# Page numbers kept in registers, a probability read moved behind the key pages, and two block transposes moved behind a projection's additions

## The chip, the cores and the metric

The kernel runs on one core of one Trainium2 chip. The core has a matrix engine (TensorE, PE in the profile), a vector engine (VectorE, DVE), a scalar engine (ScalarE, ACT), a general engine (GpSimd, POOL) and a synchronization engine (SyncE, SP) that here only issues transfers and loads registers. Each engine works through its own queue in order; engines wait for each other, and for transfers, through semaphores. The metric is the time of one execution in device microseconds (us); lower is better.

## The reference

A transformer-like block in two layers, all in float32, for 8 sequences of 128 tokens with 512 features:

```python
x = x + ffn0(cond0(x))      # per-sequence 512x512 weight; then base matrix + mixture of 8 low-rank experts, top 2
x = x + ffn1(cond1(x))      # attention over a paged cache; then 64 experts of rank 8, top 16

def cond1(x):               # 32 query heads, 8 key/value heads, head size 128
    q, k, v = x @ Wq.T, x @ Wk.T, x @ Wv.T
    q, k = rope(rmsnorm(q) * qw, pos), rope(rmsnorm(k) * kw, pos)   # pos = cache_seqlens + token
    kc, vc = k_cache[block_table], v_cache[block_table]             # 16 pages of 32 keys a sequence
    scores = q @ concat(kc, k).T / sqrt(128)                        # 512 cached + 128 own keys
    scores = where(cached key index < cache_seqlens, scores, -1e30)
    return (softmax(scores) @ concat(vc, v)) @ Wo.T
```

## The kernel before

The first layer runs first (to about 130 us), the last layer's feed-forward part partly at the end. In between stands a main loop over 64 units, and the change lies there. A unit is one sequence and one key/value head with its four query heads. Units are ordered by step: step `st` is one sequence and one pair of key/value heads, and its two units are `u = 2*st` (first turn) and `u = 2*st + 1` (second turn). All engines are scheduled by hand: the order in which the program writes the instructions is the order in each engine's queue. `iteration(u)` writes one turn of the loop, and it works on several units at once:

- `scores(u, h)` for the four heads h (L439: 512 cached keys, L442: 128 own keys), into one of two PSUM buffers that alternate; `mask_exp` (DVE L452 masks and finds the row minimum, ACT L463 takes the exponential); `normalize` (DVE L468 takes the reciprocal of the row sum, POOL L469 scales the row).
- `blocks(u, h)` (DVE L474) transposes a head's probabilities in blocks of 32x32 into the buffer `pb`; `blocks_qk(u + 2, u)` (DVE L425) does the same for the rotated queries and keys of unit u + 2, in the same buffer. There is one `pb`: it is written for a unit after the exchange of the unit before has read it.
- `exchange_out(u)` (L486) writes `pb` to a buffer px in DRAM, two transfers from SP and two from ACT, 400 KB each. `exchange_in(u - 1)` reads px back in the transposed arrangement: `qkb` (L1000, 320 KB: queries and keys of unit u + 1) and `pT` (L1003, 1280 KB: probabilities of unit u - 1). `heads_qk` (ACT L1010) then makes `qkT` for the next unit's scores. `values(u - 2)` (PE L1023) multiplies the probabilities with the cached values at the end of the turn.
- `gather(st + 1, ...)` reads the key pages of the next step, 16 pages of 32 KB, eight in each turn. For each page SP loads the page's number from SBUF into a register (L192, TENSOR_LOAD) and issues the transfer with it (L193, packets of 256 bytes). Five pages stand ahead of `exchange_in`, three behind it. `gather_v` reads values from POOL.
- `project` (PE L262) computes the query, key and value projections of later units by a seven-product scheme, three or four products a turn. In the slots of heads 1, 2 and 3 it takes `slots[h - 1]`; DVE adds each product to its partial sums (L265). Turns with u%4 = 3 or 1 take products 1, 2, 6 and 7, the others 4, 5 and 3. Product 5 (slot of the third head, h = 2) needs two additions, product 2 one.
- `output(u - 3, h)` (PE L1148) multiplies earlier results with the output weight into the PSUM bank `y`; `add_output` (DVE L1217) adds it to the accumulators, the late part after the last `blocks`. `rotate(u + 3)` (DVE L329 to L347) follows it, and it waits for the factors `rs` that `norms` computes on ACT (L311) and POOL (L315, L317).

POOL also carries weight sums (L163, L1098), loads of weights (`load_q`, L153, in turns with u%16 from 7 to 12, between the scaling of the third and of the fourth head) and the gathers of values. Within one head's slot, PE's order is scores, output, projection. In the slot of the third head DVE's order before the change is: mask step of head 2, reciprocal of head 1, `blocks_qk`, `blocks(u, 0)`, the projection's additions; the mask step of head 3 follows.

Of the kernel before, what the change touches and what calls it, by code (L numbers as in the profile page):

```python
# [17 lines left out]
B = 8  # L18
# [8 lines left out]
PAGES, PSIZE, NPP = 64, 32, 16  # L27
# [3 lines left out]
GH = 2  # L31
# [27 lines left out]
def adaln_ffn_kernel(  # L59
# [25 lines left out]
    nc = tc.nc  # L85
# [20 lines left out]
    pg = const.tile([1, B * NPP], I32, name="pg")  # L106
# [70 lines left out]
        for i, to in parts:  # L177
            nc.gpsimd.dma_start(out=wo_t[:, to], in_=wo[hf, i])

    kv_t = {}  # L180

    def gather(step, first=0, end=NPP):
        hf, b = divmod(step, B)
        if first == 0:
            kv_t[step] = (
                kvp.tile([P, NPP, GH, PSIZE], F32, tag="kt", name=f"kt_{step}"),
                kvp.tile([P, LC, GH * D], F32, tag="vt", name=f"vt_{step}", bufs=3),
            )
        kt, vt = kv_t[step]
        for j in range(first, end):  # L190
            at = b * NPP + j
            page = nc.sync.value_load(pg[0:1, at : at + 1])  # L192
            nc.sync.dma_start(  # L193
                out=kt[:, j, :, :].rearrange("p g t -> p (g t)"),
                in_=kc[hf, ds(page, 1)].rearrange("o p f -> p (o f)"),
            )
# [30 lines left out]
    NU = len(units)  # L227
# [176 lines left out]
    mask_t, px_t, qkb_t = {}, {}, {}  # L404
# [18 lines left out]
    def blocks_qk(u, w):  # L423

        nc.vector.transpose(  # L425
            pb_t[w][:, :, PW:].rearrange("p i (h a) -> p h i a", a=32),
            qk_t.pop(u).rearrange("p h t d -> p h (t d)").rearrange(
                "p h (i a) -> p h i a", a=32
            ),
        )  # L430
# [35 lines left out]
    def normalize(u, h):  # L466
        den = den_t.pop((u, h))
        nc.vector.reciprocal(den, den)  # L468
        nc.gpsimd.tensor_scalar(p_t[u, h], p_t[u, h], den, 1.0, ALU.mult, ALU.mult)  # L469

    def blocks(u, h):

        w = (LC + 1) * 32
        nc.vector.transpose(  # L474
            pb_t[u][:, :, h * w : (h + 1) * w].rearrange("p i (j a) -> p j i a", a=32),
            p_t.pop((u, h)).rearrange("p (j i a) -> p j i a", i=QD, a=32),
        )

    def exchange_out(u):

        pb = pb_t.pop(u)
        m = dram_x.tile([QD, 32, QD, XW], F32, tag="px", name=f"px_{u}")
        w = XW if u + 2 in range(4, NU) else PW
        for i in range(QD):
            eng = nc.sync if i < QD // 2 else nc.scalar
            eng.dma_start(  # L486
                out=m[:, :, i, :w].rearrange("k b f -> b k f"),
                in_=pb[i * 32 : (i + 1) * 32, :, :w],
            )
        px_t[u] = m  # L490
# [501 lines left out]
    with ExitStack() as l1:  # L992
        wk1 = l1.enter_context(tc.tile_pool(name="l1_1", bufs=1))
        wk2 = l1.enter_context(tc.tile_pool(name="l1_2", bufs=2))

        def exchange_in(u):
            m = px_t.pop(u).rearrange("k b i f -> (k b) i f")
            if u + 2 in range(4, NU):
                qkb = wk1.tile([P, QD, NH * 32], F32, tag="qkb", name=f"qkb_{u + 2}")
                nc.sync.dma_start(out=qkb, in_=m[:, :, PW:])  # L1000
                qkb_t[u + 2] = qkb
            pT = wk1.tile([P, QD, PW], F32, tag=f"pT{u % 2}", name=f"pT_{u}")
            nc.sync.dma_start(out=pT, in_=m[:, :, :PW])  # L1003
            pT_t[u] = pT
# [287 lines left out]
        def room(b):  # L1292
            at = [0]

            def sb(n, shape):
                if n in ("yT", "zg", "zT"):
                    v = room_t[n, b if n != "yT" else b % 2]
                    return v if len(shape) == 2 else v.rearrange("p (c s) -> p c s", c=shape[1])
                at[0] += -(-shape[1] // 8) * 8
                return room_t["small", b % 2][:, at[0] - -(-shape[1] // 8) * 8 :][:, : shape[1]]  # L1300

            def psum(n, shape):
                late = n == "tp" and b >= 4
                t = banks(f"ftp_{b}") if late else bank("kv" if n == "z" else "q", f"f{n}_{b}")
                if len(shape) == 2:
                    return t[:, : shape[1]]
                t = t[:, : shape[1] * shape[2]]
                return t.rearrange("p (c s) -> p c s", c=shape[1])

            return sb, psum  # L1310
# [107 lines left out]
        def iteration(u):  # L1418
            nonlocal room2

            on = lambda v: 0 <= v < NU
            fb = LAST.get(u)
            r, group = u % 16, (u // 16 + 1) * GH
            f = room(fb) if fb is not None else None

            if u % 4 == 3:
                k, j, four = (u + 5) // 4, 0, True
            elif u % 4 == 0:
                k, j, four = (u + 4) // 4, 0, False
            elif u % 4 == 1:  # L1430
                k, j, four = (u + 3) // 4, 1, True
            else:
                k, j, four = (u + 2) // 4, 1, False
# [4 lines left out]
            pages = on(u) and 1 < st + 1 < NQ * B  # L1438
# [1 line left out]
            if pages:  # L1440
                gather(st + 1, first, first + 5)
            if on(u - 1):
                exchange_in(u - 1)
            if pages:
                gather(st + 1, first + 5, end)
            if pages:
                gather_v(st + 1, u % GH * LC // GH, (u % GH + 1) * LC // GH)
            if on(u + 3) and u % GH == 1 and u > 1:
# [38 lines left out]
            for h in range(REP):  # L1487
                if on(u):
                    if (u, h) not in ((1, 0), (1, 1), (2, 0)):
                        scores(u, h)  # L1490
                        mask_exp(u, h)
                    if h > 0 and (u, h) != (1, 1):
                        normalize(u, h - 1)

                    if (u, h) == (1, 2):
                        transpose_qk(3)

                    sums_o(u, h)
                    sums_w(u, h)
                    if 16 <= u < NU - 8 and (r, h) == (2, 3):  # L1500
                        load_o(u // 16, (1, B12))

                    if h == 2:
                        new_pb(u)
                        if u + 2 in range(4, NU):
                            blocks_qk(u + 2, u)
                    if h > 1:
                        blocks(u, h - 2)
                    if h == 1 and u == NU - 5:
                        f_fold()  # L1510
                    if u == NU - 5 and h == 1:
                        t4 = wo_t[:, 6, : 2 * (E1 + HN)].rearrange("p (c n) -> p c n", c=2)
                        fw_t["qa"], qa_steps[:] = quarters_of(
                            fw_t["a"],
                            *quarter_rooms(wo_t[:, 5]),
                            t4[:, :, E1:],
                            t1_room.rearrange("p (c n) -> p c n", c=2),
                        )
                        sa = fw_t["sa"]
                        fw_t["qa"][M1], fw_t["qa"][M2] = (sa[:, c : c + 2, : E1 + HN] for c in (0, 2))  # L1520
                        fw_t["qa"][M4] = t4
                    at = (u - NU + 5, h)
                    if at == (1, 0):
                        nc.vector.tensor_copy(fw_t["qa"][M4][:, :, :E1], fw_t["s"][:, 2:])
                    if at in ((0, 1), (0, 2), (1, 0), (1, 1)):
                        qa_steps.pop(0)()
                    if u in GATED and h == 1:
                        f_add(GATED[u])
                    if u in GATED and h == 2:
                        f_mult(GATED[u])  # L1530
                    if h == 3:
                        z_blocks(u)
                    if h == 2 and u in FIRST:
                        f_turn_of(2 * FIRST[u])
                    if u in REST:
                        if h == 1:
                            f_turn_of(2 * REST[u] + 1)
                        elif h > 1:
                            f_step(REST[u], 2 * h - 4, 2 * h - 3)
                elif u in GATED and u < NU + 2:  # L1540
                    if h == 1:
                        f_add(GATED[u])
                    elif h == 2:
                        f_mult(GATED[u])
                    elif h == 3:
                        z_blocks(u)
                if on(u - 3):
                    output(u - 3, h)
                    sums_a(u - 3, h)
                if u in REST and h == 3:  # L1550
                    f_rest_products(REST[u], 0)
                if h > 0 and slots:
                    project(k, j, slots[h - 1 : h])

                if (u, h) in WHOLE:
                    project_whole(1, *WHOLE[u, h])
            if on(u - 3):
# [19 lines left out]
            if on(u):  # L1577
                blocks(u, REP - 2)
                blocks(u, REP - 1)
                exchange_out(u)  # L1580
            if on(u - 3):
                add_output(u - 3, True)
            if 16 <= u < NU - 8 and r in (0, 1, 2):
                n = u // 16
# [192 lines left out]
```

## Time and profile before

| what | value |
|---|---|
| time, median of 3 executions | 1198.89 us (1198.29 to 1201.55) |
| the profiled execution, its own time | 1203.57 us |
| span of the profiled execution, first to last instruction | 1201.8 us |
| granted TensorE clock in it | 1.00 |
| busy: PE, DVE, ACT, POOL | 99%, 78%, 42%, 64% of the span |
| mean busy share of the DMA engines by queue: SP's, ACT's, POOL's | 53.2%, 13.4%, 12.5% |
| the chain of waits, by engine | PE 82%, DMA 5%, DVE 4%, POOL 4%, issue 2%, SP's queue 2%, ACT 1% |
| transfers, issue to landing (median): kt, px, qkb, pT | 4.8, 5.5, 3.6, 7.3 us |

A group of instructions in the profile is named by its line, engine, operation and tiles (out<-in). "Idle before" is the time for which the engine stood idle just before the instruction, with what ended it. The view of waits lists, for an engine, who waited for whom, the total, the number of times and the longest one. In the order of time, each line gives start, duration, engine, line, operation and tiles; neighbouring instructions of one group are merged (x5 is five of them, and the duration then runs from the first's start to the last's end). SPq is SP's sequencer. Ends of matmuls are modelled.

### The profile page before, as it was taken

The page shows a single profiled execution, that of the slowest core. Times are in us where ns is not written, and L with a number is a line of the kernel's source. Part 1 is how long each engine was busy: PE and PEld are TensorE (multiplying, and loading weights), DVE is VectorE, ACT ScalarE, POOL GpSimd, SP SyncE. Part 2 cuts the span into 40 slices and gives each one's busy share as a digit, 9 for nine tenths or more (in the row PEclk, how much of TensorE's full clock was granted, in tenths as well). Part 3 has the DMA queues.
Part 4 walks back from the last instruction along what each step waited for, and adds up shares of the span by engine and source line. Part 5 has one row for each costly group of instructions (what it writes and reads, how often), then busy time and mean ns, then how long its engine had stood idle before and what let it go on. Part 6 is the DMA issues. An engine that isn't in the chain of part 4 may idle for free.

```text
span 1201.8 us, 17007 instructions
## 1 busy us (share of the span) xinstructions
PE 1188.7 (99%) x4196; PEld 721.8 (60%) x4196; DVE 936.6 (78%) x2141; ACT 509.3 (42%) x1469; POOL 771.6 (64%) x867
## 2 busy tenths in 40 slices
PE   9999999999999999999999999999999999999998
PEld 7766555565655556555555555565655555655567
DVE  2557788787978887878888787878888888897757
ACT  1345544444444444434444344444444444444321
POOL 3554879778746676678656685677656684765432
PEclk9999999999999999999999999999999999999999
DMA  8823787888779978898889978888789878888643
GB/s 316 312 72 119 249 248 241 265 281 281 235 248 262 322 239 272 269 287 273 248 254 286 276 241 282 284 272 267 245 256 303 274 249 252 270 289 262 197 153 114
DMA packets 205447, 302.35 MB, mean 252 GB/s; under 512 B 84771, under 2 KB 119332, under 8 KB 204324
## 3 DMA queue, kind: packets, MB, share of 16 engines
q1 hardware_dynamic: 170164, 196.29, 53.2%
q10 hardware_dynamic: 18864, 52.57, 13.4%
q0 software_dynamic: 16320, 52.40, 12.5%
q8 instruction: 34, 0.56, 0.2%
q14 instruction: 65, 0.53, 0.1%
HBM read 185.44 MB, written 115.74 MB: 251 GB/s over the span
## 4 chain that ended last, share of the span: by engine, by line
PE 82%; DMA 5%; DVE 4%; POOL 4%; issue 2%; SPq 2%; ACT 1%; ACTq 0%; DVEq 0%; POOLq 0%
PE o L1023 18%; PE p L262 17%; PE s L439 15%; PE y L1148 12%; PE s L442 4%; DMA kt<-in_kc 3%; PE p L295 3%; PE cp L627 2%; PE bp L649 2%; PE y L1161 2%; DMA px<-pb 2%; DVE pb L474 1%; POOL p L469 1%; SPq L192 1%; PE op L981 1%
## 5 line engine op out<-in xcount | busy, mean ns | idle before, releaser
L463 ACT ACTIVATE p<-p,low 128x640 f32<-128x640 f32 x256 | 211.9, 828 | 428.5 <-DVE den L468 268.9
L469 POOL TENSOR_SCALAR p<-p,den 128x640 f32<-128x640 f32 x256 | 210.2, 821 | 219.5 <-DVE den L468 218.3
L452 DVE CUSTOM_DVE_ANT_0 p<-s,mask,rs 128x640 f32<-128x640 f32 x256 | 222.8, 879 | 82.8 <-PE s L442 82.0
L262 PE MATMUL p<-wqkv,xo 128*128 128x384 f32 x784 | 281.0, 487 | 1.3 <-POOL wqkv L163 0.7
L439 PE MATMUL s<-kt,qkT 128*128 128x512 f32 x504 | 258.3, 594 | 4.7 <-DMA px<-pb 1.7
L1023 PE MATMUL o<-pT,vt 128*128 128x512 f32 x512 | 230.3, 592 | 0.0
L474 DVE STREAM_TRANSPOSE pb<-p 128x640 f32<-128x640 f32 x248 | 204.8, 826 | 24.8 <-POOL p L469 24.7
L1148 PE MATMUL y<-wo,oT 128*128 128x256 f32 x784 | 206.5, 380 | 1.2 <-DVE yp L1217 1.0
L262 PEld LDWEIGHTS p<-wqkv,xo 128*128 128x128 f32 x784 | 148.3, 190 | 70.7 <-POOL wqkv L163 1.9
L442 PEld LDWEIGHTS s<-qkT 128*128 128x128 f32 x504 | 95.8, 190 | 120.5 <-issue 120.5
L203 POOL DMA_INDIRECT vt<-in_vc,vrow x128 | 138.3, 1081 | 42.0 <-issue 30.1
L1023 PEld LDWEIGHTS o<-pT,vt 128*128 128x128 f32 x512 | 97.0, 190 | 108.0 <-issue 92.8
L439 PEld LDWEIGHTS s<-kt,qkT 128*128 128x128 f32 x504 | 94.5, 190 | 77.1 <-issue 33.9
L1148 PEld LDWEIGHTS y<-wo,oT 128*128 128x128 f32 x784 | 131.9, 191 | 10.1 <-PE s L442 1.5
L311 ACT ACTIVATE sq<-c 128x128 f32<-128x128 f32 x320 | 98.8, 309 | 9.5 <-DVE oT L474 1.4
L442 PE MATMUL s<-qkT 128*128 128x128 f32 x504 | 96.8, 274 | 0.0
L317 POOL TENSOR_TENSOR rs<-ss,mhalf 128x5 f32<-128x5 f32 x64 | 84.0, 1312 | 5.3
L1046 ACT COPY oT<-o 128x512 f32<-128x512 f32 x64 | 37.5, 585 | 111.0 <-PE o L1023 92.4
L315 POOL TENSOR_SCALAR ss<-ss,eps 128x5 f32<-128x5 f32 x64 | 23.4, 366 | 73.1 <-ACT sq L311 73.1
L265 DVE TENSOR_TENSOR c<-c,p 128x384 f32<-128x384 f32 x84 | 44.9, 534 | 26.7 <-PE p L262 26.7
L1023 PE MATMUL o<-pT,vn 128*128 128x512 f32 x128 | 65.4, 592 | 0.0
L425 DVE STREAM_TRANSPOSE pb<-ca 128x640 f32<-128x640 f32 x60 | 49.9, 832 | 14.5 <-DMA kt<-in_kc 8.9
(301 smaller groups left out, 1513.8 us busy)
## 6 DMA issues: line engine op xcount, KB each, us to landing
pT<-px SPq DMA_DIRECT2D x64, 1280.0 KB, 7.3
px<-pb SPq DMA_DIRECT2D x120, 400.0 KB, 5.5
px<-pb ACTq DMA_DIRECT2D x120, 400.0 KB, 5.5
qkb<-px SPq DMA_DIRECT2D x60, 320.0 KB, 3.6
kt<-in_kc SPq DMA_DIRECT2D x512, 32.0 KB, 4.8
wqkv<-in_wqkv POOLq DMA_DIRECT2D x32, 384.0 KB, 5.1
wo<-in_wo POOLq DMA_DIRECT2D x17, 512.0 KB, 7.7
yd<-yp POOLq DMA_DIRECT2D x12, 512.0 KB, 9.1
```

Of the source, the lines that this page charges most:

```text
L203: nc.gpsimd.indirect_dma_start(out=kv_t[step][1][:, c, :], out_offset=None, in_=vc, in_offset=bass.IndirectOffsetOnAxis(ap=vrow[:, hf, at ...
L262: nc.tensor.matmul(out=ps, lhsT=xo[:, pr, x, c, :], rhs=w[:, c, :], start=(c == 0), stop=(c == 1))
L311: nc.scalar.activation(sq, cs[:, at : at + D], AF.Square, accum_out=ss[:, h : h + 1])
L317: nc.gpsimd.tensor_tensor(rs, ss, mhalf, ALU.pow)
L439: nc.tensor.matmul(out=s[:, :L], lhsT=qkT[:, h, :], rhs=kt[:, :, g % GH, :], start=True, stop=True)
L442: nc.tensor.matmul(out=s[:, L:NK], lhsT=qkT[:, h, :], rhs=qkT[:, REP, :], start=True, stop=True)
L452: nc.vector.tensor_tensor_reduce(out=p, in0=s_t.pop((u, h))[:, :NK], in1=mask_t[st], scale=rs_t[u][:, h : h + 1], scalar=BIG, op0=ALU.add, ...
L463: nc.scalar.activation(p, p, AF.Exp, bias=low, scale=-1.0, accum_out=den)
L469: nc.gpsimd.tensor_scalar(p_t[u, h], p_t[u, h], den, 1.0, ALU.mult, ALU.mult)
L474: nc.vector.transpose(pb_t[u][:, :, h * w : (h + 1) * w].rearrange("p i (j a) -> p j i a", a=32), p_t.pop((u, h)).rearrange("p (j i a) -> ...
L1023: nc.tensor.matmul(out=o, lhsT=vt[:, c, j * D : (j + 1) * D] if c < LC else vn_t.pop(u), rhs=pT[:, c], start=(c == 0), stop=(c == LC),)
L1148: nc.tensor.matmul(out=y_t["y"][:, half * HN : (half + 1) * HN], lhsT=part(key)[:, i * S : (i + 1) * S], rhs=wo_t[:, slot(w, key[0] // (B ...
```

## The change

Three things are changed. First, the numbers of the first five pages of a turn (turns 5 to 61) are loaded into registers at the end of the turn before, ahead of `exchange_out`, instead of each just ahead of its transfer; the loads themselves stay as many. Second, `exchange_in` is split: the read of `qkb` keeps its place behind the first five pages, and the read of `pT` stays right behind it in first turns, but goes behind the turn's last three pages in second turns. Third, in units 4 to 58, `blocks_qk(u + 2, u)` and `blocks(u, 0)` are written after the projection of the third head's slot, so that DVE's order there is: mask step of head 2, reciprocal of head 1, the projection's additions, `blocks_qk`, `blocks(u, 0)`.

```diff
@@ -177,7 +177,12 @@
         for i, to in parts:
             nc.gpsimd.dma_start(out=wo_t[:, to], in_=wo[hf, i])
 
-    kv_t = {}
+    kv_t, page_t = {}, {}
+
+    def page_number(step, j):
+
+        at = step % B * NPP + j
+        page_t[step, j] = nc.sync.value_load(pg[0:1, at : at + 1])
 
     def gather(step, first=0, end=NPP):
         hf, b = divmod(step, B)
@@ -188,8 +193,9 @@
             )
         kt, vt = kv_t[step]
         for j in range(first, end):
-            at = b * NPP + j
-            page = nc.sync.value_load(pg[0:1, at : at + 1])
+            if (step, j) not in page_t:
+                page_number(step, j)
+            page = page_t.pop((step, j))
             nc.sync.dma_start(
                 out=kt[:, j, :, :].rearrange("p g t -> p (g t)"),
                 in_=kc[hf, ds(page, 1)].rearrange("o p f -> p (o f)"),
@@ -993,12 +999,15 @@
         wk1 = l1.enter_context(tc.tile_pool(name="l1_1", bufs=1))
         wk2 = l1.enter_context(tc.tile_pool(name="l1_2", bufs=2))
 
-        def exchange_in(u):
-            m = px_t.pop(u).rearrange("k b i f -> (k b) i f")
+        def exchange_queries(u):
+            m = px_t[u].rearrange("k b i f -> (k b) i f")
             if u + 2 in range(4, NU):
                 qkb = wk1.tile([P, QD, NH * 32], F32, tag="qkb", name=f"qkb_{u + 2}")
                 nc.sync.dma_start(out=qkb, in_=m[:, :, PW:])
                 qkb_t[u + 2] = qkb
+
+        def exchange_in(u):
+            m = px_t.pop(u).rearrange("k b i f -> (k b) i f")
             pT = wk1.tile([P, QD, PW], F32, tag=f"pT{u % 2}", name=f"pT_{u}")
             nc.sync.dma_start(out=pT, in_=m[:, :, :PW])
             pT_t[u] = pT
@@ -1440,9 +1449,13 @@
             if pages:
                 gather(st + 1, first, first + 5)
             if on(u - 1):
-                exchange_in(u - 1)
+                exchange_queries(u - 1)
+                if u % GH == 0 or not pages:
+                    exchange_in(u - 1)
             if pages:
                 gather(st + 1, first + 5, end)
+            if on(u - 1) and u % GH and pages:
+                exchange_in(u - 1)
             if pages:
                 gather_v(st + 1, u % GH * LC // GH, (u % GH + 1) * LC // GH)
             if on(u + 3) and u % GH == 1 and u > 1:
@@ -1502,9 +1515,10 @@
 
                     if h == 2:
                         new_pb(u)
-                        if u + 2 in range(4, NU):
+                    behind = h == 2 and 3 < u < NU - 5
+                    if h > 1 and not behind:
+                        if h == 2 and u + 2 in range(4, NU):
                             blocks_qk(u + 2, u)
-                    if h > 1:
                         blocks(u, h - 2)
                     if h == 1 and u == NU - 5:
                         f_fold()
@@ -1552,6 +1566,10 @@
                 if h > 0 and slots:
                     project(k, j, slots[h - 1 : h])
 
+                if on(u) and behind:
+                    blocks_qk(u + 2, u)
+                    blocks(u, 0)
+
                 if (u, h) in WHOLE:
                     project_whole(1, *WHOLE[u, h])
             if on(u - 3):
@@ -1577,6 +1595,9 @@
             if on(u):
                 blocks(u, REP - 2)
                 blocks(u, REP - 1)
+                if 3 < u < NU - GH - 1:
+                    for n in range(5):
+                        page_number((u + 1) // GH + 1, (u + 1) % GH * (NPP // GH) + n)
                 exchange_out(u)
             if on(u - 3):
                 add_output(u - 3, True)
```

## The prediction

> **What bounds the kernel now.** I read the page's busy shares first, then TensorE's waits, then the order of time on SP and DVE. A unit u (one sequence, one head group) is one turn of the main loop; its start below is the first score matmul (L439).
>
> ```profile
> PE 1188.7 (99%) x4196; PEld 721.8 (60%) x4196; DVE 936.6 (78%) x2141; ACT 509.3 (42%) x1469; POOL 771.6 (64%) x867
> ```
>
> TensorE is full. Unit starts in its timeline are 15.94, 17.23, 14.21 and 17.23 us apart for u%4 = 2, 3, 0, 1 wherever nothing waits (64.61 us for four), and most units hit these to 0.1 us. So only what exceeds them can be won. Units 5 to 58 exceed them by 8.0 us: 0.62 at 17/18, 2.30 at 27 to 30, 0.35 at 33/34, 1.43 at 35/36, 1.93 at 41/42, 1.39 at 45. TensorE's waits name the ends:
>
> ```profile
> PE s L439 <- DMA px<-pb: 1.7, 1, 1.7
> PE s L439 <- DMA kt<-in_kc: 1.6, 2, 1.2
> PE y L1148 <- DVE yp L1217: 1.0, 1, 1.0
> PE p L262 <- POOL wqkv L163: 0.7, 1, 0.7
> ```
>
> The first, at 778.39 us, is also a page wait: the last key packets (the 256-byte packets of SP's queue) ended at 777.34, and no score start in the trace stands less than 1.0 us behind the last one. By this edge the units ending at 17, 33, 35 and 41 all lose their time to key pages, with the small restart after each: 0.62 + 0.35 + 1.43 + 1.93 = 4.33 us. Eight more of the 30 page sets land within 0.6 us of the edge. SP before that wait:
>
> ```profile
> 761.52 5.80 SPq L193 DMA_DIRECT2D kt<-in_kc  x5
> 767.87 0.54 SPq L1000 DMA_DIRECT2D qkb<-px  x1
> 768.46 0.62 SPq L1003 DMA_DIRECT2D pT<-px  x1
> 769.61 2.63 SPq L193 DMA_DIRECT2D kt<-in_kc  x3
> ```
>
> Three pages stand behind the 1280 KB pT read; the last landed 6.05 us after its issue at 771.29.
>
> DVE in unit 32 (start 614.10), the part that is reordered:
>
> ```profile
> 619.69 0.89 DVE L452 CUSTOM_DVE_ANT_0 p<-s,mask,rs 128x640 f32<-128x640 f32 x1 [0.53 <-PE s L442]
> ...
> 620.58 0.83 DVE L425 STREAM_TRANSPOSE pb<-ca 128x640 f32<-128x640 f32 x1
> 621.33 0.80 DVE L474 STREAM_TRANSPOSE pb<-p 128x640 f32<-128x640 f32 x1
> 622.05 0.52 DVE L265 TENSOR_TENSOR c<-c,p 128x384 f32<-128x384 f32 x1
> 622.49 0.54 DVE L265 TENSOR_TENSOR c<-u,p 128x384 f32<-128x384 f32 x1
> 622.96 0.87 DVE L452 CUSTOM_DVE_ANT_0 p<-s,mask,rs 128x640 f32<-128x640 f32 x1
> ...
> 624.58 0.52 DVE L265 TENSOR_TENSOR c<-c,p 128x384 f32<-128x384 f32 x1
> ...
> 626.09 0.85 DVE L474 STREAM_TRANSPOSE pb<-p 128x640 f32<-128x640 f32 x1 [0.18 <-POOL p L469]
> 626.86 1.18 DVE L1217 TENSOR_TENSOR yp<-yp,y 128x1024 f32<-128x1024 f32 x1
> ```
>
> Here DVE has no gap: the two transposes fill the time until the projection at 619.92 to 621.37 is done.
>
> **pT behind the pages (odd u).** The three pages move ahead of pT's issue (0.62 us) and of its 1280 KB. Page sets landed 3.3 to 6.05 us after the last issue, so 0.6 us earlier is sure and up to some 3 us likely; the waits are 0.4 to 1.9 us long, so all four close. Price: 4.33 us in the profiled execution (1203.57 us, span 1201.8 and 1.8 around it). That execution is 4.68 us over the median 1198.89, and the runs differ by 3.26 among themselves; TensorE's work is the same, so waits differ, and transfers are what varies. The bounds for the median are therefore 0 and 4.33. I take two thirds, 2.9, since the edge is met or nearly met in 12 of 30 page sets, too many for one execution's accident. pT comes later by three issues of 0.84 us less about 0.6 that the read before it gains: 1.9 us. Its use is a whole unit later (values, 19 us after the issue), so itself it costs nothing.
>
> Its bytes end later, though, and run into the next exchange: pT issued at 605.13 ended at 611.95 and the next px packets began at 612.76, so 0.8 us of room becomes about 0.8 of overlap. By these rows px lands about 1.1 us later in even units (0.3 of it from DVE, below). In u%4 = 0 units its packets now end 4.7 to 6.0 us in and free the buffer some 0.5 later; with 1.1 that is 6.3 to 7.6. Needed there is 8.2 (below): nothing. The Trainium skill speaks against this move: "DMA: Bandwidth & Descriptors", section "Two DMAs through the same engine are not ordered", has descriptors of one queue start in order, so SP's half of px would stand wholly behind a later pT. By that rule the landing moves the full 1.9 us and DVE's 0.3, to 7.4 to 8.7, and the latest would just be felt.
>
> **Page numbers in registers.** 285 of 512 register loads (L192, 0.26 to 1.69 us, median 0.277) leave the stretch behind the px issue, where one takes about 1 us, for SP's idle time before the next px: 5 x 0.33 = 1.65 us, while SP idles from 608.3 to 611.9 in unit 31 and 2.4 us in unit 41. That hides them; without this cover px would leave late by the rest. SP then reaches qkb some 2 to 4 us sooner, but qkb waits for px: in unit 41 the fifth page went at 766.99 and px freed DVE's buffer at 767.85, qkb was issued at 767.87. So qkb gains 0 to 1 us, and the scores that need it have 2.8 to 5 us of room in regular units: nothing on TensorE. The first five pages issue sooner into px's time: 160 KB beside its 1600 KB, as now, so 0 to 0.6 us on px; I take 0, since three of the five are in it already. The waiting qkb holds pT and three pages behind it, as before.
>
> **Additions first (u = 4 to 58).** No instruction is added; DVE gives up the filler. In unit 32 the additions go to 621.4 to 622.4, then the transposes to 623.9, and the fourth head's mask step moves from 622.96 to 623.80: +0.84. It carries to the last transpose and to L1217 (end 628.04 to 628.88), since behind it only 0.18 us is idle. For u%4 = 1 and 3, the projection ends 8.58 us in; the same working gives +0.4 and +0.3 at the unit's end, and for u%4 = 2 +0.8. On ACT the fourth exponential is as late; behind it in order stand the qkT copy, the squares of the norms and ACT's half of px. POOL's rs follows the squares, and DVE's rotation waits for rs (0.49 us in unit 32), so the next unit's first mask step comes about 0.8 later too; the third score has 1.41 us of room for that (0.88 after units 8, 24, 40): free.
> Who waits: y (L1148) of the next unit, 1.08 us after its start. After u%4 = 0 units the room is 1.35 us, elsewhere 1.5 to 2.7. Regular: 1.35 - 0.84 = 0.51 remains, free (unit 13: 1.00). After units 8, 24 and 40 the room is 0.23 to 0.25, because two weight-load issues (1.58 us) stand on POOL between the third and the fourth head's scaling; the third's reciprocal is 0.84 late, so POOL is too: 3 x (0.84 - 0.24) = 1.8 us lost. Unit 5 already waits 0.21 us on DVE's mask step at its third score: +0.8. Unit 52 has 0.56 there: +0.3. Sum +2.9, bounds 1.5 (half absorbed) and 5 (jitter eats the 0.5 elsewhere).
> What it wins: blocks_qk waits for px landing 14.5 us in all, longest in units 28 (1.80) and 41 (1.16). In unit 28 the additions can run in that wait, at 554.9 instead of 557.7, so everything behind comes 0.9 earlier and the y wait at 564.14 (1.04) nearly closes. Unit 45's y gap gives 0.1: -1.0, bounds 0 and -2.3 (all of 27 to 30). Unit 45's weight wait stays: POOL.
>
> **Sum.** -2.9 - 1.0 + 2.9 = -1.0: 1202.6 against the profiled 1203.57, so **1197.9** against the median 1198.9. I call 0.3% (3.6 us) what a measurement of this kernel can tell from no change.
>
> **Rivals.**
> 1. Faster: all 4.33 us of page waits are in ordinary executions too, units 27 to 30 lose their whole 2.3, and the costs come to 2.0. -4.6: 1194.3. For: twelve page sets at the edge. Against: the lowest run, 1198.29, lies 5.3 below the profiled one already. 0.24.
> 2. Slower, one mechanism: DVE ends u%4 = 0 units too late for y. It decides from the point where blocks_qk starts over 8.2 + 0.5 = 8.7 us into such a unit, that is if px lands 1.1 us later than the latest above. At 9.5, eleven units (eight regular, and 9, 25, 41) lose 0.8: 8.8 - 1.0, 1206.7. For: the delayed pT and the later px add up, and this unit type is the shortest. Against: px now ends 4.7 to 6.0 in. A partial form gives 1202.5 to 1204. 0.26.
> 3. The order does not help: 256-byte packets set the landing, not pT. Then only the 0.62 us of issue time counts, the short waits at 17 and 33 close and 0.6 of each other: about -1.5 (two thirds taken) - 1.0 + 2.9, 1199.3, within 0.3%. 0.08.
> The forecast itself, 1195.5 to 1202.3: 0.42.
>
> **Numbers.** Faster 0.24; within 0.3% 0.42 + 0.08 = 0.50; slower 0.26. The range 1194.0 to 1204.0 takes in the faster case and the partial slower form, leaving about 0.1 at each end.
>
> **What would show it.** Right: the last three pages land under 4 us after issue and no score waits for kt or px at odd-even borders; units keep 15.94/17.23/14.21/17.23; L425 starts about 1.8 us later than now in u%4 = 0; y waits of about 0.6 us open units 9, 25 and 41; the y wait of 29 shrinks. Wrong: page waits remain, y waits in every u%4 = 1 unit, or score waits on qkT.

## The result, and the profile after

The changed kernel took 1208.25 us (median, 1205.42 to 1211.06) against 1201.05 us before on the same chip: a ratio of 1.0059, 95% interval 1.0045 to 1.0074. It is 0.6% slower. Forecast were 1197.9 us, with a range of 1194.0 to 1204.0 and a chance of 0.26 for slower. The profiled execution took 1211.06 us, with a span of 1209.3 (before: 1203.57 and 1201.8). One execution each of two kernels below, `even_only` (6606.41 us) and `odd_and_4` (5052.90 us), took over four times as long as all others and is left out of the medians and ratios.

TensorE's waits in the changed kernel. The lines moved by the edit: L445 is the score matmul (was L439), L458 the mask step (L452), L1157 y (L1148), L1226 the additions of y (L1217), L1244 the copy of y that stands for one of them in some units (L1235), L268 the projection (L262), L271 its additions (L265), L431 `blocks_qk` (L425), L480 `blocks` (L474), L475 the scaling on POOL (L469), L317 to L323 the norms (L311 to L317), L1019 the copy to qkT (L1010).

```profile
PE s L445 <- DVE low L458: 6.1, 5, 3.6
PE y L1157 <- DVE yp L1226: 2.2, 4, 0.9
PE p L268 <- POOL wqkv L163: 1.7, 2, 1.2
...
PE y L1157 <- DVE yp L1244: 0.9, 1, 0.9
...
PE s L445 <- ACT qkT L1019: 0.4, 1, 0.4
```

Both waits that the page edits were aimed at, for px (1.7 us) and for kt (1.6 us), are gone. In their place stand waits for DVE: scores for a mask step, y for its addition. SP's queue ahead of unit 42, where before the last page landed 6.05 us after its issue:

```profile
763.60 6.07 SPq L199 DMA_DIRECT2D kt<-in_kc  x5
770.24 0.55 SPq L1006 DMA_DIRECT2D qkb<-px  x1
771.29 2.02 SPq L199 DMA_DIRECT2D kt<-in_kc  x3
773.41 0.53 SPq L1012 DMA_DIRECT2D pT<-px  x1
```

The three pages (x3) now stand ahead of pT (L1012). In units 5 to 57 the last page lands 1.3 to 3.0 us after its issue (3.3 to 6.05 before), and the scores have 2.6 us or more behind it (1.0 to 3.6 before).

DVE in unit 32, which now starts at 617.34. Columns are start, duration, engine, line, operation and tiles, and in brackets the idle time ahead:

```profile
622.94 0.89 DVE L458 CUSTOM_DVE_ANT_0 p<-s,mask,rs 128x640 f32<-128x640 f32 x1 [0.53 <-PE s L448]
...
624.66 0.56 DVE L271 TENSOR_TENSOR c<-c,p 128x384 f32<-128x384 f32 x1 [0.75 <-PE p L268]
625.13 0.55 DVE L271 TENSOR_TENSOR c<-u,p 128x384 f32<-128x384 f32 x1
625.60 0.84 DVE L431 STREAM_TRANSPOSE pb<-ca 128x640 f32<-128x640 f32 x1
626.36 0.80 DVE L480 STREAM_TRANSPOSE pb<-p 128x640 f32<-128x640 f32 x1
627.30 0.88 DVE L458 CUSTOM_DVE_ANT_0 p<-s,mask,rs 128x640 f32<-128x640 f32 x1
...
630.44 0.84 DVE L480 STREAM_TRANSPOSE pb<-p 128x640 f32<-128x640 f32 x1 [0.18 <-POOL p L475]
631.21 1.18 DVE L1226 TENSOR_TENSOR yp<-yp,y 128x1024 f32<-128x1024 f32 x1
```

The 0.75 us of idle time ahead of L271 is new: before, the two transposes lay there. The fourth head's mask step (627.30) comes 9.96 us into the unit, where it came 8.86 in (622.96 with the start at 614.10), and the last transpose ends at +13.94 instead of +12.84: 1.10 us later.

Where the 7.5 us of span went, by the unit starts of the two traces: 1.2 us less up to unit 5 (start 174.30 before, 173.08 after), 4.0 more over units 5 to 58 (879.98 before, 884.01 after), 4.7 more in units 59 and 60 together (31.83 before, 36.54 after), nothing behind them. Of the 4.7, some 1.7 us are lost to a stretch at half clock behind the long wait in unit 60 (last section).

### The profile page after: what moved, and what is told of

Same layout as the page of the kernel before. It is cut to its first block, busy times and chain, and to the rows that moved or that the text cites. A ratio compares the mean times of both kernels' runs of the same rounds, so it can differ in the third digit from the quotient of the medians.

```text
span 1209.3 us, 16984 instructions
## 1 busy us (share of the span) xinstructions
PE 1192.3 (99%) x4196; PEld 722.2 (60%) x4196; DVE 940.5 (78%) x2141; ACT 504.0 (42%) x1469; POOL 771.4 (64%) x867
## 4 chain that ended last, share of the span: by engine, by line
PE 75%; DMA 8%; DVE 5%; POOL 5%; issue 3%; ACT 2%; SPq 1%; ACTq 0%; DVEq 0%; POOLq 0%
PE p L268 16%; PE o L1032 16%; PE s L445 14%; PE y L1157 11%; DMA px<-pb 5%; PE s L448 3%; PE p L301 3%; PE cp L633 2%; PE bp L655 2%; PE y L1170 2%; DMA qkb<-px 2%; POOL p L475 1%; ACT sq L317 1%; DVE pb L480 1%; DVE p L458 1%
## 5 line engine op out<-in xcount | busy, mean ns | idle before, releaser
L469 ACT ACTIVATE p<-p,low 128x640 f32<-128x640 f32 x256 | 211.3, 826 | 475.3 <-DVE den L474 292.9
L475 POOL TENSOR_SCALAR p<-p,den 128x640 f32<-128x640 f32 x256 | 210.2, 822 | 222.3 <-DVE den L474 221.0
L268 PE MATMUL p<-wqkv,xo 128*128 128x384 f32 x784 | 281.3, 487 | 1.7 <-POOL wqkv L163 1.7
L445 PE MATMUL s<-kt,qkT 128*128 128x512 f32 x504 | 259.6, 597 | 6.7 <-DVE low L458 6.1
L458 DVE CUSTOM_DVE_ANT_0 p<-s,mask,rs 128x640 f32<-128x640 f32 x256 | 221.5, 881 | 49.1 <-PE s L448 40.5
L480 DVE STREAM_TRANSPOSE pb<-p 128x640 f32<-128x640 f32 x248 | 204.7, 826 | 25.0 <-POOL p L475 24.9
L1157 PE MATMUL y<-wo,oT 128*128 128x256 f32 x784 | 206.8, 380 | 3.1 <-DVE yp L1226 2.2
L268 PEld LDWEIGHTS p<-wqkv,xo 128*128 128x128 f32 x784 | 148.1, 190 | 71.7 <-POOL wqkv L163 3.6
L445 PEld LDWEIGHTS s<-kt,qkT 128*128 128x128 f32 x504 | 94.3, 190 | 80.1 <-issue 25.1
L1157 PEld LDWEIGHTS y<-wo,oT 128*128 128x128 f32 x784 | 131.8, 191 | 12.7 <-PE s L448 4.1
L317 ACT ACTIVATE sq<-c 128x128 f32<-128x128 f32 x320 | 98.8, 309 | 9.5 <-DVE oT L480 1.4
L323 POOL TENSOR_TENSOR rs<-ss,mhalf 128x5 f32<-128x5 f32 x64 | 85.0, 1328 | 5.3
L271 DVE TENSOR_TENSOR c<-c,p 128x384 f32<-128x384 f32 x84 | 45.5, 541 | 37.3 <-PE p L268 37.3
L271 DVE TENSOR_TENSOR c<-u,p 128x384 f32<-128x384 f32 x84 | 46.1, 548 | 30.2 <-PE p L268 30.2
```

The lines of the kernel that those rows point to most:

```text
L268: nc.tensor.matmul(out=ps, lhsT=xo[:, pr, x, c, :], rhs=w[:, c, :], start=(c == 0), stop=(c == 1))
L271: add = lambda out, a: nc.vector.tensor_tensor(out, a, ps, ALU.add)
L317: nc.scalar.activation(sq, cs[:, at : at + D], AF.Square, accum_out=ss[:, h : h + 1])
L445: nc.tensor.matmul(out=s[:, :L], lhsT=qkT[:, h, :], rhs=kt[:, :, g % GH, :], start=True, stop=True)
L458: nc.vector.tensor_tensor_reduce(out=p, in0=s_t.pop((u, h))[:, :NK], in1=mask_t[st], scale=rs_t[u][:, h : h + 1], scalar=BIG, op0=ALU.add, ...
L469: nc.scalar.activation(p, p, AF.Exp, bias=low, scale=-1.0, accum_out=den)
```

## Experiments

Two theories stood at the start. A: the additions-first order is the loss, because it leaves DVE idle in every unit. B: the loss comes from pT standing behind the pages, so from later reads and exchanges. Each run is compared with the kernel before on the same chip; its medians there were 1201.82 us for the four parts, 1201.01 us for `odd_only`, `spare_y`, `early_end` and `only_4_of_8`, and 1200.39 us for the other four. The ratios are estimated from the single executions and are not the quotients of the medians.

### The parts alone

Four kernels take the change apart. Only the page edits (sp_only), with DVE's old order:

```diff
-                    behind = h == 2 and 3 < u < NU - 5
+                    behind = h == 2 and False
```

> Both edits on SP (page numbers ahead, pT behind the pages in second turns), DVE's old order. Theory A (the additions-first order on DVE is the whole loss, SP's edits win): the page waits of the before profile go (4.3 us in units 5 to 58, 1.2 in unit 3), nothing is added: 3 to 5.5 us faster than before. Theory B (pT behind the pages pushes the px exchange, and the late px costs DVE): 4 to 8 us slower than before, with blocks_qk waiting for px longer than 14.5 us in all, and the long wait at unit 60.

Only the additions first (dve_only): the early `page_number` calls are left out, and `exchange_in(u - 1)` stands right behind `exchange_queries(u - 1)` in both turns.

> Additions first on DVE alone, SP as before. Theory A: it loses what the whole change loses and the page waits besides: 8 to 13 us slower than before, y waits of 0.8 us at units 9, 25 and 41, and waits at 5, 13, 29 and 60. Theory B: within 2 us of before, no long wait at unit 60.

Only pT behind the pages (pt_only), and only the registers (reg_only):

> Only pT behind the pages in second turns; register loads and DVE as before. Theory A: the page waits go by this edit alone, 3 to 5 us faster. Theory B: 3 to 8 us slower. If the registers matter, this is over 1 us from the kernel with both SP edits.

> Only the page numbers loaded ahead. Both theories: qkb waits for px anyway, so within 1 us of before; the last pages are issued 0 to 1 us earlier, which takes up to 2 us of the page waits away. If SP's earlier page transfers push px, 1 to 3 us slower.

| kernel | median, us | ratio to before, 95% interval |
|---|---|---|
| sp_only | 1201.37 | 0.9990 [0.9975, 1.0005] |
| dve_only | 1215.72 | 1.0121 [1.0095, 1.0146] |
| pt_only | 1204.27 | 1.0018 [1.0001, 1.0035] |
| reg_only | 1200.65 | 0.9986 [0.9971, 1.0000] |

Of the four expectations only that of the registers came near. The page edits together met neither theory (3 to 5.5 us faster, or 4 to 8 slower), the order alone lost 1.21%, 14.5 us, where A had 8 to 13, and pT alone lost 0.18%, 2.2 us, where A had it 3 to 5 us faster and B 3 to 8 slower.

The order alone loses 1.2%, twice what the whole change loses. Its waits on TensorE:

```profile
PE s L445 <- DMA kt<-in_kc: 7.8, 7, 1.5
PE y L1157 <- DVE yp L1226: 2.3, 4, 0.9
```

The page waits went from 1.6 us (and 1.7 put down to px) to 7.8, of which 1.5 stand at the start of unit 4, ahead of the first reordered slot. In this kernel the exchange leaves 0.6 to 1.1 us later in every kind of unit (medians), so qkb and pT, which wait for it on SP, and the three pages behind them come later too, and the pages were already at the edge. On top of the page edits the same order costs 1.0059 - 0.9990 = 0.69%, 8.3 us: with the edits to SP's queue no page wait is left, and that part of its price is gone. So the order is a loss by itself and on top of the page edits, which is theory A.

The page edits alone win nothing that this measurement can tell from no change, though their page waits are gone as well. The traces show a cost that stands against the win: DVE idles ahead of `blocks_qk` (L431), waiting for px, for 31.0 us in all, against 14.5 before; in units with u%4 = 2 for 9.5 us against 1.4. (The view puts about half of it down to key pages, which this transpose does not read; they share SP's queue.) The parts tell whose it is: 36.3 us with pT alone, 13.6 with the registers alone. That is B's mechanism, and in the old order it reaches TensorE in a few places (of the 2.7 us, 0.5 were there before, in units 5 and 60):

```profile
PE s L445 <- DVE low L458: 2.7, 5, 1.1
PE y L1157 <- DVE yp L1226: 1.9, 4, 0.8
```

In the whole change the same idle time is 6.0 us, since the additions run while px is on its way. So the order hides most of a cost that the moved pT creates, and creates another one.

### Where the new order costs

The additions first in odd units alone and in even units alone, and the whole change again for a second profile:

```diff
-                    behind = h == 2 and 3 < u < NU - 5
+                    behind = h == 2 and 3 < u < NU - 5 and u % 2
```

> The whole change, but the additions come first in odd units alone (5 to 57). Theory A: even units, where product 5 needs two additions, end 1 us earlier again, so the y waits of 9, 25 and 41 (3.3 us) go, and with unit 58 in the old order the wait of unit 60 (4.7 us) goes: 1200 to 1201.5. Rival (the old order waits for px as in the run of both page edits without the new order, 30.9 us of waits ahead of the transposes): even units wait for px again, y waits at 20/21, 29, 41 and 45 come back, 1202 to 1204.

> The whole change, but the additions come first in even units alone (4 to 58): the complement of the run with odd units alone, which took 1201.31 against 1201.37 for both page edits without the new order. Theory A (the loss sits in even units, where product 5 needs two additions and the unit's end moves back 1 us or more): 1207 to 1208.5, as much as the whole change, with y waits at 9, 25 and 41, a weight-sum wait at 43 and the late exchange of unit 58. Rival (the shift of one unit is handed to the next, so both kinds are needed for the loss): 1203 to 1205, the average of the two.

> The changed kernel once more, for a second profile. If its loss is by the program: y waits of about 0.86 us at units 9, 25 and 41 and weight-sum waits at 27 and 43 come at the same places, and no page wait; if unit 60's score wait of 3.6 us is one too, it is there again, else it is one execution's late transfer. Time 1207 to 1210 by either.

| kernel | median, us | ratio to before, 95% interval |
|---|---|---|
| odd_only | 1201.31 | 1.0000 [0.9988, 1.0013] |
| even_only | 1207.10 | 1.0045 [1.0029, 1.0061] |
| after_again | 1208.68 | 1.0057 [1.0037, 1.0078] |

Against the page edits alone (0.9990), odd units cost 0.10%, even units 0.55%, both together 0.69%: the parts add up, within intervals of about 0.15% to each side. The loss sits in the even units. Their third slot has two additions to bring forward, the odd ones' has one; that this is what tells them apart was not tested by itself. TensorE's waits between 200 and 1060 us, even units alone:

```profile
PE y L1157 <- DVE yp L1226: 2.1, 4, 0.9
PE p L268 <- POOL wqkv L163: 1.7, 2, 1.2
PE y L1157 <- DVE yp L1244: 1.7, 2, 0.9
```

and odd units alone:

```profile
PE p L268 <- POOL wqkv L163: 1.4, 2, 0.7
PE y L1157 <- DVE yp L1226: 0.9, 1, 0.9
```

The second profile of the whole change (span 1209.0) repeats these places to 0.01 us: y waits of 0.86, 0.85 and 0.86 us in units 9, 25 and 41, weight-sum waits of 0.45 and 1.21 us in units 27 and 43. Those are the program's. The wait in unit 60 is there again, but with 1.79 us instead of 3.63, and unit 5's is 2.56 instead of 1.32: their sizes belong to the execution.

### Two places taken out

```diff
-                    behind = h == 2 and 3 < u < NU - 5
+                    behind = h == 2 and 3 < u < NU - 5 and u % 16 != 8
```

> The whole change, but units 8, 24 and 40 keep the old order (transposes ahead of the additions). Theory A (the additions-first order costs by pushing the end of DVE's unit back, and where the room is short TensorE waits for y): the y waits of 1.09 us that open units 9, 25 and 41 go, 3 x 1.09 = 3.3 us less than the whole change's 1208.25: about 1205. The two exchanges at those units leave 1.1 us earlier besides. Rival (with both page edits the old order only waits longer for px): the transposes of these units wait for px instead, y stays late, and the time stays at 1208.

The edit also takes in unit 56 (56%16 = 8); unit 57 loses nothing in either kernel's profile. Measured: 1203.81 us, 1.0025 [1.0012, 1.0038], so 0.34% or 4.1 us less than the whole change. Expected were 3.3. In the profile the y waits of 9 and 25 are gone; the one of 41 is still there (0.86 us), and ahead of it unit 40's `blocks_qk`, back in the old order, waited 1.0 us for px, which fits the rival's mechanism in one of three places. The two waits that went are worth 2.2 us with their restarts. This profile cannot account for the rest: its execution (1208.76 us) was the slowest of the twelve, and its units 5 to 58 took 886.4 us, more than in the whole change's first profile (884.0) and less than in its second (887.3), with weight-sum waits of 1.20 us in unit 27 and 0.75 in unit 45, and 2.02 us for the mask step in unit 5. That the kernel is faster is shown by the times; that all of it comes from these three units' y waits is not.

```diff
-                    behind = h == 2 and 3 < u < NU - 5
+                    behind = h == 2 and 3 < u < NU - 9
```

> The whole change, but the additions-first order ends with unit 54 instead of 58. Theory C (the last exchange in the new order, of unit 58, leaves 1 us late and lands in unit 59, which is back in the old order; its transposes wait 2.7 us, and unit 60, which also carries the feed-forward gate on DVE, passes it on): the exchange of unit 58 leaves at 14.6 us of its unit, the score wait of 3.6 us in unit 60 goes, units 59 and 60 take 15.8 + 16.1 us instead of 15.2 + 21.4: 2 to 4.7 us less than 1208.25, about 1204.5. Rival (any switch from the new order to the old one loses): the loss moves to units 55 and 56, and the time stays at 1207 to 1209.

Measured: 1206.68 us, 1.0045 [1.0030, 1.0061]: 0.14% less, 1.7 us, a little under the 2 to 4.7 that theory C gave, and with intervals that overlap. Units 59 and 60 take 31.8 us together, as before the change, and unit 60's score wait is 0.35 us. Nothing moved to units 55 and 56. So the loss is absent where theory C said it would be, but the theory is not confirmed: `even_only` and `spare_y` keep the new order in unit 58, as the whole change does, and their units 59 and 60 take 32.0 and 31.7 us, no more than before (31.8); `only_4_of_8` has unit 58 in the old order, and there they take 34.3, with a wait of 2.35 us in unit 60. The whole change's two profiles have 36.5 and 32.7. A large loss here needs a late px in that execution; what the end of the new order adds to it stays open.

How the 4.7 us of the first profile came about is seen on its DVE (unit 59 starts at 1057.09, unit 60 at 1072.27):

```profile
1066.87 0.84 DVE L431 STREAM_TRANSPOSE pb<-ca 128x640 f32<-128x640 f32 x1 [2.72 <-DMA px<-pb]
...
1076.04 0.35 DVE L349 SCALAR_TENSOR_TENSOR ca<-c,rs,tab 128x128 f32<-128x128 f32 x1 [1.37 <-POOL rs L323]
...
1077.50 0.22 DVE L884 COPY rooms<-fq 128x64 f32<-128x64 f32 x1
...
1081.01 0.88 DVE L458 CUSTOM_DVE_ANT_0 p<-s,mask,rs 128x640 f32<-128x640 f32 x1
...
1081.95 0.88 DVE L458 CUSTOM_DVE_ANT_0 p<-s,mask,rs 128x640 f32<-128x640 f32 x1
```

Unit 58, the last in the new order, issues its exchange at 1056.75, 15.6 us into the unit (14.6 before), and the last packet of px ends 9.5 us later, where it took 7.5 us before and 6.7 in the second profile. Unit 59 is in the old order, and its transposes wait 2.72 us. The rotation then waits for rs, and the feed-forward gate, written into this turn (L884 to L908), puts 3.5 us more ahead of unit 60's first mask step. The third score needs the buffer that this step empties.

### Versions that pick units

Three more kernels use the new order only where a run had shown a late px or no loss.

> The whole change, but the additions come first only in units 4, 12, 20, ... 52 (u%8 = 4), seven units, of which 20, 28, 36 and 44 let the transposes wait 1 to 2 us for px when both page edits are made alone (1201.37). Theory A with its other half (the new order wins where px is late and loses elsewhere): the y waits of 29 and 45 (0.83 + 0.41) shrink, nothing is added: 1199.5 to 1201. Rival (px of these units leaves later by 1 us, so the next unit's transposes and pages are later): 1202 to 1203.

> The whole change, but the additions come first only in odd units and in u%8 = 4, from unit 7 to unit 53: where the runs showed no loss by it, or a late px. Theory A: no y waits at 9, 25, 41, the px waits of units 20, 28, 36, 44 covered, 1199 to 1200.5. Rival (what odd units win is what they lose): 1201 to 1202.

> The same with u%4 = 3 and u%8 = 4 alone, from unit 7 to unit 52: in u%4 = 3 the additions move the exchange 0.6 us, the least of the four kinds. Theory A: 1199 to 1200.5. Rival (units with u%4 = 1 then wait for px as in the old order): 1201 to 1202.

| kernel | median, us | ratio to before, 95% interval |
|---|---|---|
| only_4_of_8 | 1202.13 | 0.9999 [0.9984, 1.0015] |
| odd_and_4 | 1203.30 | 1.0012 [0.9996, 1.0029] |
| three_and_4 | 1201.87 | 1.0005 [0.9991, 1.0020] |

All three expectations of 1199 to 1201 failed. Two medians lie in the range of their rival, that of `odd_and_4` above both ranges; by the ratios none of the three can be told from the kernel before. Where a y wait closes, others stay or open: the kernel with odd units and u%8 = 4 still waits 2.0 us for POOL's weight sums and 1.8 for y. No kernel here is faster than the one before by more than its interval; the nearest is the register edit alone.

## Why the prediction was wrong

By the runs the change is +0.59%, 7.1 us, where the sum had -1.0: the page edits -1.2 us instead of -2.9, and the additions first +8.3 us instead of +2.9 - 1.0. The step that failed is the second, the cost of the additions first ("Sum +2.9, bounds 1.5 and 5"): the delay on DVE was too small in the working, and POOL's queue behind it was left out.

**Page waits: the mechanism was right, the landing too, the price was not shown.** The pages land under 3.0 us after issue where "under 4 us" was forecast, and no score waits for kt or px. Of the 2.9 us priced for it, though, the page edits by themselves show 0.1% or 1.2 us, with an interval that holds zero, and pT alone, which was to bring all of it, is 2.2 us slower than before. The later px itself was sized well: in the traces its last packet ends a median of 6.20 us into units with u%4 = 0 (8 to 56), against 5.00 before; that is near the 1.1 us of the working and not the 2.2 of its second reading. "Needed there is 8.2 (below): nothing" is true for the new order, in which `blocks_qk` starts at +8.26 us in u%4 = 0 units, and the whole change waits 0.1 us in all of these. In the old order the need is at +6.48, and there the page edits wait 5.6 us. So the new order's job in this change is to pay for the moved pT, which the prediction did not see as a debt.

The prediction looked at u%4 = 0 alone. Units 18 to 20 lose 2.0 and 1.7 us in the two profiles of the whole change, 0.08 before and with the registers alone, and 0.3 to 2.2 in every profile with the moved pT. In the first profile ACT and DVE show how:

```profile
401.60 0.72 ACT L1019 COPY qkT<-qkb 128x640 f32<-128x640 f32 x1 [1.60 <-DMA qkb<-px]
406.06 0.35 DVE L349 SCALAR_TENSOR_TENSOR ca<-c,rs,tab 128x128 f32<-128x128 f32 x1 [1.87 <-POOL rs L323]
```

The queries land late, ACT's copy waits for them and the squares of the norms stand behind the copy; so rs is late, DVE's rotation waits for it, and the third score of unit 19 waits 0.64 us for a mask step that stands behind the rotation.

**Registers: right in part.** The loads now take about 0.27 us each. The time behind the px issue is not won: there the page issues themselves are now slow, 6.07 us for five in the lines above (5.80 before, with the loads among them). Alone the edit is worth 0.14%, with an interval that ends at no change. The prediction gave it nothing, which that interval allows.

**Additions first: the term that was mis-sized.** The sum had +2.9 - 1.0 us, with bounds of 1.5 and 5 on the first; the runs give 0.69%, 8.3 us, for the order on top of the page edits. The traces show two places where it fails, and a third that stays open.

- The shift itself. The working had the fourth head's mask step of unit 32 at 9.70 us into the unit (+0.84); it came at 9.96 (+1.10), behind the whole of the second transpose. In units 9, 25 and 41 the prediction had 0.24 us of room and so 0.6 us of loss each. The y waits are 1.10 - 0.24 = 0.86 us, and with the restart behind them each unit loses 1.09: 3.3 us instead of 1.8. The places were named rightly, and the run that spares them is 4.1 us faster. Unit 13, for which the working had 1.00 us of room, loses another 0.48.
- Who else waits for the fourth head. The prediction followed the rs chain to DVE's rotation and called it free. The same chain holds POOL's own queue:

```profile
792.35 0.80 POOL L475 TENSOR_SCALAR p<-p,den 128x640 f32<-128x640 f32 x1 [2.76 <-DVE den L474]
793.09 0.80 POOL L153 DMA_DIRECT2D wqkv<-in_wqkv  x1
793.94 0.80 POOL L475 TENSOR_SCALAR p<-p,den 128x640 f32<-128x640 f32 x1
796.23 1.22 POOL L321 TENSOR_SCALAR ss<-ss,eps 128x5 f32<-128x5 f32 x1 [1.49 <-ACT sq L317]
797.54 1.20 POOL L323 TENSOR_TENSOR rs<-ss,mhalf 128x5 f32<-128x5 f32 x1
```

  This is the turn from unit 42 to 43 (start 795.97). The scaling of the third head waits for DVE's reciprocal, and a weight-load issue (L153) stands ahead of the fourth's. The rs operation comes at +1.57 us, where it came at -0.92 before. Behind it stand the gathers of values and three weight sums (L163); the last sum ends at +14.36 instead of +11.87, and the projection waits 1.21 us for one of them. Before, with unit 43 starting at 794.41:

```profile
793.13 0.27 POOL L315 TENSOR_SCALAR ss<-ss,eps 128x5 f32<-128x5 f32 x1 [0.95 <-ACT sq L311]
793.49 1.20 POOL L317 TENSOR_TENSOR rs<-ss,mhalf 128x5 f32<-128x5 f32 x1
```

  From the start of unit 42 the fourth head's scaling comes 0.9 us later than before, rs 2.4; 0.95 of it is that the first of the two small operations took 1.22 us instead of 0.27, in both profiles of the change, for which the traces name no cause. Unit 27 is the same kind (0.45). Together that is 1.7 us of waits which the prediction did not have; the 0.7 us that unit 45 waited for a weight sum before are gone in this profile. The wait in unit 43 is there with the order alone (1.20 us) and not with the page edits alone. No kernel takes this out by itself, so its share of the time is read from the traces and not shown by a run.
- Units 59 and 60, behind the end of the new order, with the feed-forward gate: 4.7 us in one profile of the whole change, 0.9 in the other, and nothing in two other kernels with the same order in unit 58. Ending the order earlier gave 1.7 us, with intervals that overlap. The prediction did not look at the turn where the edit stops; whether it had to is not shown.

**The win in unit 28** (-1.0) is real in kind: its y wait in unit 29, 1.04 us before, fell to 0.31. Unit 29 still loses 0.71.

**Rival 2** had the right sign and the right engine, but its condition did not come about. It needed `blocks_qk` to start later than 8.7 us into u%4 = 0 units and eleven units to lose 0.8 us each. `blocks_qk` starts at +8.25 or +8.26 in nine of fourteen of them and at +8.74 at the latest, and the regular ones keep about 0.2 us. Besides the three units already named, y is waited for in 29 and 45 (0.31 and 0.17 us). Its "partial form" up to 1204 was still too small.

## What to carry to other kernels

When an instruction that fills a wait is moved away, the time it filled comes back as idle time wherever nothing else fills the wait; follow that delay through every queue that has the late result in its order (here ACT's squares, then POOL's gathers and weight sums), not only to the engine that uses it next. An order that covers one wait can pay for a transfer that another part of the same change made later, so price the parts alone and together. Before a wait in one profile is put down to the edit, look for it in a second profile and in kernels with and without that part of the edit: the long wait of unit 60 was not tied to it.

## What the runs showed of the hardware

In the main loop the granted TensorE clock fell to half at the end of single waits of 2.0 to 3.6 us. Around the 3.63 us wait of unit 60, in stretches of 4 us (time, length, busy times by engine, then granted clock, DMA share and GB/s):

```profile
1078.00:1082.00 4.00, 0.37 (x2) 0.05 (x1) 3.62 (x17) 0.83 (x3) 1.90 (x2) 1.00 0.96 332
1082.00:1086.00 4.00, 4.00 (x7) 1.86 (x8) 2.75 (x9) 2.60 (x6) 2.73 (x3) 0.57 0.83 255
1086.00:1090.00 4.00, 4.00 (x12) 1.93 (x11) 2.85 (x6) 1.35 (x5) 1.23 (x3) 1.00 0.73 254
```

and behind the 2.56 us wait of unit 5 in the second profile of the same kernel:

```profile
179.40:182.80 3.40, 3.36 (x7) 2.15 (x8) 1.77 (x6) 2.10 (x5) 3.37 (x5) 0.50 0.88 271
```

Each time the clock stood at 0.50 for 3.4 us, which is 1.7 us of full clock. In the main loops of this case's profiles five waits of 2.02, 2.26, 2.35, 2.56 and 3.63 us were followed by it, two of 1.99 and 2.81 us were not, and none of 1.8 us or less was. The Trainium skill ("TensorE: Matmul & The Clock Gate", section "What's actually happening") has the drop after at least one idle window of about 3.4 us, the return after a busy window of about that length, and calls the window free-running; the 3.4 us at half clock agree, but here 2.02 us of waiting were enough, and 2.81 us once were not. So here a wait of over 2 us of a TensorE that is 99% busy cost 1.7 us more than its length in five of seven cases.
